# Softmax sums on 32 rows, an earlier start of the input loads, and norms on ScalarE in a four-layer convolution kernel

## The chip, the cores and the metric

The kernel runs on one core of one Trainium2 chip. It is a single program that is launched once; the metric is its device time in microseconds (us), and the time shown for a kernel is the median over several executions. TensorE (PE in the profile) multiplies matrices out of the on-chip buffer SBUF into the accumulator memory PSUM; VectorE (DVE), ScalarE (ACT) and GpSimd (POOL) do elementwise work; SyncE (SP) issues most DMA transfers between the chip's main memory and SBUF. Each engine takes its instructions in the order of its own queue, and waits at the head of the queue until what the instruction needs is there.

## What is computed

The input is x, 4 images of 384 channels and 64 x 64 positions in float32. Four layers follow, each a group norm (32 groups of 12 channels), a block and a residual addition. The change touches layers 0 and 1 alone; layers 2 and 3 (a gated depthwise block with batch norms, and a depthwise 7 x 7 convolution with kernels made from the data) are the same code before and after.

```python
# layer 0: x = x + L0(group_norm(x))
x_attn, x_skip = x[:, :96], x[:, 96:]
xn  = layer_norm_over_channels(x_attn) * ln_w + ln_b
qkv = bn(einsum('oc,bchw->bohw', w_qkv, xn))          # 16 + 16 + 96 channels
attn = softmax(einsum('bcn,bcm->bnm', q, k) * scale)  # over all 4096 positions
out  = einsum('bcn,bmn->bcm', v, attn)
xm = relu(concatenate([out, x_skip], axis=1))
y  = bn(einsum('oc,bchw->bohw', w_proj, xm))

# layer 1: x = x + L1(group_norm(x))
t = einsum('bchw,oc->bohw', x, w_in)
t = irfft2(rfft2(t in 8 x 8 patches) * fft_filter)
t = depthwise_3x3(t, w_dw)
g = gelu(t[:, :192]) * t[:, 192:]
y = einsum('bchw,oc->bohw', g, w_out)
```

## The kernel before

**Tiling.** The 384 channels lie as NJ = 3 groups of 128 partitions (P), the 4096 positions of an image as eight blocks of 512 columns. One image is called a batch, numbered 0 to 3. The attention works on the first 96 channels (PD), the other 288 are the skip channels.

**The whole program.** `phase_a` does layers 0 and 1, and is what the change edits; layers 2 and 3 follow. `phase_a` first loads constants and weights and makes the projection weights (`qkv_weights`). From these weights a bound on the scores is worked out (`score_bound`); it is compared with a limit, and the result, the one integer `large`, is read into a register in `score_shifts` (L637), where every engine branches on it (L638). Only if it is 1 are the maxima of the scores computed; in the runs here it is 0 and the branch jumps over them. Then `x_norm(0)` loads batch 0 in 24 pieces of 256 KB on SP's queue (L565) and takes its group-norm statistics, and `qkv(0)` makes queries, keys and values. Then, for each batch b, `side_by_side` interleaves the steps of `attention(b)` with `others`: the statistics of batch b+1, layer 1 of batch b-1, and queries, keys and values of batch b+1. Last comes layer 1 of batch 3, which has no attention beside it; the code calls it `alone`, and from its 21st piece on it is interleaved with loads for layer 2 (`strips_of`).

**Order.** The Python order gives each instruction its priority; a tile scheduler then sets the order on each engine, with the scores raised (`high_priority`, L693). Tiles come from pools in which a tag has a number of buffers: a new tile of a tag waits until the oldest one of that tag is no longer read. The PSUM tags are "s" (one tile of four banks: the scores `sc_s`, and in the last batch `taps_m`), "a" (two banks: `av` and `rd_m`; in the last stage the output products `out_m1`) and "m" (two banks: everything taken by `pm`).

**A step of attention.** For query block i and key group c (eight of each), `scores` makes four products of 32 rows each into `sc_s`, and ScalarE takes two exponentials of 128 x 1024 into `probs` (L703). Four products with `vt` add into `av` (L734). `vt` has 97 columns for each 128 keys: 96 value channels and one column of ones, so that row 96 of `av` becomes the softmax's sum. In the products the matrix called weights (loaded into PE first) is `vt`, and `probs` streams through it.

**The end of a block.** One step into the next block (c == 1) `finish(av)` copies `av` through a Relu to `av_up` on ScalarE (L715), VectorE takes the reciprocal of row 96 (L717), PE spreads that one row over 96 rows by a product with a row of ones (`rd_m`, L719), and VectorE multiplies `av_up` with it (L720) into rows 0 to 95 of `xm`. `layer0_end` loads the residual block (`x_res`), fills the skip channels of `xm` on ScalarE (L756, L760), makes nine products for the projection (`proj_m`, L767), adds bias and residual on VectorE (L774), takes statistics and stores the block.

**Layer 1** takes a block of eight rows of the image (a band) as four tiles of 16 columns. For each tile `tile_norm` normalizes three groups on VectorE (L826, `xb`); `tile_hidden` multiplies by w_in (`t_m`, L841) and ScalarE copies (`t_t`, L849); `tile_filter` goes to Fourier coefficients (`coef_m`, L856) and multiplies by the filter on VectorE (L858); `tile_back` goes back (`back_m`, L867) and ScalarE writes the tile into the band (L869). `band_taps` then does the 3 x 3 depthwise convolution: nine taps for each of three groups, tap 0 on ScalarE and eight on VectorE as multiply-and-add (L918). In the `alone` case the first TAPS = 3 taps of a group are made on PE instead, as products with diagonal matrices (L907, built on POOL in `tap_weights`), and VectorE starts from their sum in `taps_m`. Two Gelus and two multiplies give the gate, and `band_out` multiplies by w_out, adds the residual and stores.

**At the start,** `layer_norm` loads a block of x (`ln_x`), normalizes it (L578), centres it by a product, squares it on ScalarE into `ln_rs` (L587; tag "lr", two buffers), averages by a product, takes the root and multiplies. `qkv` then makes `q_m`, `k_m` and the values `v_m` (L625: four products, each with 97 columns of `wv`), copied to `vt` on VectorE (L626).

Of the kernel before, what the change touches and what calls it, by code (L numbers as in the profile page):

```python
# [37 lines left out]
TAPS = 3  # L38
# [187 lines left out]
class _Builder:  # L226
# [154 lines left out]
    def qkv_weights(self, pool):  # L381
# [4 lines left out]
        w = pool.tile([P, PD], F32, tag="wq_raw", name="wq_raw")  # L386
# [7 lines left out]
        wt = pool.tile([PD + 1, P], F32, tag="wq_t", name="wq_t")  # L394
        raw = pool.tile([PD, P], F32, tag="wq_rawt", name="wq_rawt")
# [9 lines left out]
        self.wv = pool.tile([PD + 1, PD + 1], F32, tag="wv", name="wv")  # L405
# [3 lines left out]
        nc.gpsimd.memset(self.wv[PD : PD + 1, PD : PD + 1], 1.0)  # L409
# [28 lines left out]
    def phase_a(self, strips):  # L438
# [3 lines left out]
        with ExitStack() as ctx:  # L442
# [12 lines left out]
            self.one = cp.tile([PD + 1, PD], F32, tag="one", name="one")  # L455
            nc.gpsimd.memset(self.one, 1.0)
            self.w_proj = self.weight(cp, "w_proj_t")
            self.w_in = self.weight(cp, "w_in_t")
            self.w_out = self.weight(cp, "w_out_t")
# [5 lines left out]
            for k in ("r0", "m0", "n0"):  # L465
                setattr(self, k, cp.tile([P, NJ, B], F32, tag=k, name=k))
            w = lambda tag, name: self.work.tile([P, C], F32, tag=tag, name=name)
# [21 lines left out]
            self.qkv_weights(cp)  # L489
            self.score_shifts(cp)  # L490
            for _ in self.x_norm(0):
                pass
# [79 lines left out]
    def layer_norm(self, b, i):  # L572
# [13 lines left out]
        rs = self.wk("ln_rs", "lr", 2)[0:PD]  # L586
# [7 lines left out]
    def qkv_tiles(self):  # L594
# [4 lines left out]
        vt = self.big.tile([P, 32, PD + 1], F32, tag="vt", name="vt", bufs=2)  # L599
        return q, k4, vt  # L600

    def qkv(self, b, q, k4, vt):
# [3 lines left out]
        for i in range(8):  # L606
# [16 lines left out]
            mv = m[:, 0 : 4 * (PD + 1)].rearrange("p (c d) -> p c d", d=PD + 1)  # L623
# [18 lines left out]
    def maxima(self, b):  # L642
# [14 lines left out]
        for i in range(8):  # L657
# [20 lines left out]
            row = self.big.tile([P, 512], F32, tag="up", name="nm_row", bufs=2)  # L678
# [4 lines left out]
    def attention(self, b, q, k4, vt):  # L683
# [27 lines left out]
        def finish(av):  # L711

            xm = self.work.tile([P, NJ, 512], F32, tag="xm", name="xm")
            up = self.big.tile([P, 512], F32, tag="up", name="av_up", bufs=2)[0 : PD + 1]
            nc.scalar.activation(up, av[0 : PD + 1], AF.Relu)  # L715
            rd = self.wk("av_rd", "rd", 1)
            nc.vector.reciprocal(rd[PD : PD + 1], up[PD : PD + 1])  # L717
            m = self.pa("rd_m")
            nc.tensor.matmul(m[0:PD, :], lhsT=self.one[PD : PD + 1, :], rhs=rd[PD : PD + 1], start=True, stop=True)  # L719
            nc.vector.tensor_mul(xm[0:PD, 0], up[0:PD], m[0:PD, :])  # L720
# [58 lines left out]
    def layer1(self, b):  # L779

        nc = self.nc
        r, gm = self.norm1[0:2]
        st = self.stats_tile("x1_st")
        alone = b == B - 1
        if alone:
# [999 lines left out]
```

## Time and profile before

| | |
|---|---|
| median of 9 executions | 5136.43 us (5120.58 to 5146.69) |
| the profiled execution | 5133.12 us, of it the profile's span 5131.4 us |
| TensorE clock granted, mean of the span | 0.947 |
| start, to 80 us: PE busy | 27.7 of 80 us |
| attention of batch 0 (80 to 690): PE, VectorE, ScalarE busy | 593.7, 217.5, 281.1 of 610 us |
| batch 1 (690 to 1230) | 521.7, 283.1, 260.2 of 540 us |
| batch 2 (1230 to 1760) | 511.7, 290.0, 257.8 of 530 us |
| batch 3 (1760 to 2290) | 519.5, 276.8, 236.0 of 530 us |
| layer 1 of batch 3 (2290 to 2610) | 284.0, 205.8, 74.8 of 320 us; clock 0.89 |
| layers 2 and 3 (2610 to the end) | 2199.1, 1394.0, 965.1 of 2521 us; clock 0.92 |

The stages' limits are read from the timeline and rounded to 10 us. In the profile an operation's row names its line, engine, operation, what it writes and what it reads; a trailing x is the number of instructions, "mean ns" the duration of one. Products are pipelined on PE, so durations of one overlap and start-to-start times say more. Between a group's busy time and the next group stands the idle time of the engine just before it and what ended most of that. In the row of slices each digit is the busy share in tenths of one fortieth of the span; PEclk is the granted clock in tenths. In a timeline a row gives start, duration, engine, line and operation, and in brackets the engine's wait before it with the instruction that ended it. In the table of windows each engine has its busy time and its number of instructions, then come granted clock, DMA share and GB/s.

### The profile page before, as it was taken

What the parts mean: (1) busy time and instruction counts of PE and PEld (TensorE: products, weight loads), DVE (VectorE), ACT (ScalarE), POOL (GpSimd) and SP (SyncE); (2) the same over time, 40 slices, a digit from 0 to 9 for tenths busy, and PEclk for the clock granted to TensorE, in tenths of its full rate; (3) what the DMA queues carried; (4) which work ended last, traced back from release to release, by engine and by line L of the source; (5) the groups of instructions that cost most, each with busy time, mean ns of one, the idle gap of its engine ahead of it and who ended that gap; (6) DMA issues with size and microseconds to landing.
All of it is one profiled execution on the core that took longest, in us unless ns stands there. A gap on an engine that the chain in (4) does not pass through costs nothing. (4 is left out here: it accounts for less than half of the span.)

```text
span 5131.4 us, 47956 instructions
## 1 busy us (share of the span) xinstructions
PE 4657.5 (91%) x17963; PEld 2569.1 (50%) x17963; DVE 2703.1 (53%) x4450; ACT 2099.1 (41%) x2753; POOL 733.9 (14%) x524
## 2 busy tenths in 40 slices
PE   5999999999999999999879999599999995559999
PEld 2333444334443343435458888344444442448999
DVE  4322456634555345565767788544421114658775
ACT  3544344454444544443135666311133334652320
POOL 1000000000000000000025555000000000125433
PEclk9999999999999999999979999799999997669999
DMA  5210211111121101113249999766643334647776
GB/s 161 72 48 28 89 56 63 60 51 43 56 71 68 38 31 62 62 68 102 70 127 283 291 297 294 237 257 241 239 180 148 147 136 182 244 161 246 220 221 190
DMA packets 387543, 723.30 MB, mean 141 GB/s; under 512 B 21628, under 2 KB 221159, under 8 KB 380391
## 3 DMA queue, kind: packets, MB, share of 16 engines
q1 hardware_dynamic: 333528, 519.50, 32.4%
q10 hardware_dynamic: 28494, 105.99, 5.2%
q0 software_dynamic: 25280, 94.65, 4.7%
q8 instruction: 145, 2.38, 0.2%
q14 instruction: 96, 0.78, 0.0%
HBM read 432.48 MB, written 287.57 MB: 140 GB/s over the span
## 5 line engine op out<-in xcount | busy, mean ns | idle before, releaser
L734 PE MATMUL av<-probs,vt 128*97 128x512 f32 x2048 | 963.1, 605 | 0.0
L703 ACT ACTIVATE probs<-sc_s 128x1024 f32<-128x1024 f32 x512 | 499.5, 1020 | 758.1 <-PE av L734 741.0
L734 PEld LDWEIGHTS av<-probs,vt 128*97 128x97 f32 x2048 | 321.7, 166 | 508.7 <-issue 505.3
L1123 PE MATMUL conv_m<-toep,z 128*128 128x256 f32 x2304 | 519.9, 385 | 12.9 <-DVE toep L1104 7.4
L918 DVE SCALAR_TENSOR_TENSOR acc<-band,vecs,acc 128x512 f32<-128x512 f32 x696 | 493.1, 746 | 42.6 <-POOL band L879 25.0
L1393 PE MATMUL h_m<-f_h,cm_w_t 128*128 128x512 f32 x1152 | 496.5, 594 | 7.9 <-ACT f_h L1383 7.9
L1123 PEld LDWEIGHTS conv_m<-toep,z 128*128 128x128 f32 x2304 | 438.7, 193 | 74.6 <-DVE z L1057 4.9
L1104 POOL TENSOR_TENSOR toep<-w,band 128x1536 f32<-128x1536 f32 x96 | 330.5, 3444 | 278.4 <-PE conv_m L1123 207.9
L1344 PE MATMUL h_s<-e_tok,cm_w_t 128*128 128x512 f32 x768 | 365.2, 599 | 5.4 <-DVE e_tok L1329 5.4
L1677 PE MATMUL conv_m<-toep,z 128*128 128x128 f32 x3072 | 364.2, 277 | 2.1 <-DVE rest_o L1685 2.1
L1393 PEld LDWEIGHTS h_m<-f_h,cm_w_t 128*128 128x128 f32 x1152 | 219.4, 191 | 284.9 <-issue 272.7
L1677 PEld LDWEIGHTS conv_m<-toep,z 128*128 128x128 f32 x3072 | 355.3, 194 | 2.6 <-issue 2.3
L695 PE MATMUL sc_s<-q,k 32*128 32x512 f32 x2048 | 301.0, 645 | 16.3 <-ACT probs L703 11.5
L841 PE MATMUL t_m<-w_in_t,xb 128*128 128x384 f32 x768 | 283.6, 502 | 6.4 <-ACT band L869 3.2
L1351 ACT COPY e_h<-h_s 128x1024 f32<-128x1024 f32 x96 | 97.2, 1012 | 419.0 <-PE h_s L1344 419.0
L767 PE MATMUL proj_m<-xm,w_proj_t 128*128 128x512 f32 x576 | 264.8, 598 | 0.8 <-DVE xm L720 0.8
L774 DVE SCALAR_TENSOR_TENSOR x_res<-proj_m,bn_c,x_res 128x512 f32<-128x512 f32 x96 | 71.8, 748 | 337.1 <-PE proj_m L767 337.0
L1344 PEld LDWEIGHTS h_s<-e_tok,cm_w_t 128*128 128x128 f32 x768 | 147.8, 193 | 192.1 <-issue 185.4
L1353 DVE BATCH_NORM_STATS2 h_st<-e_h 128x6 f32<-128x512 f32 x192 | 123.2, 685 | 185.7 <-ACT e_h L1351 185.6
L1401 DVE BATCH_NORM_STATS2 h_st<-f_h 128x6 f32<-128x512 f32 x72 | 50.0, 694 | 323.0 <-ACT f_h L1400 323.0
L841 PEld LDWEIGHTS t_m<-w_in_t,xb 128*128 128x128 f32 x768 | 142.0, 193 | 149.7 <-issue 66.1
L1344 PE MATMUL h_s<-z,cm_w_t 128*128 128x512 f32 x384 | 198.2, 599 | 12.1 <-DVE z L1329 12.1
(366 smaller groups left out, 6273.0 us busy)
## 6 DMA issues: line engine op xcount, KB each, us to landing
d<-d_o ACTq DMA_DIRECT2D x96, 512.0 KB
c_d<-d SPq DMA_DIRECT2D x96, 512.0 KB
hid<-e_h ACTq DMA_DIRECT2D x16, 3072.0 KB
f_h<-hid SPq DMA_DIRECT2D x16, 3072.0 KB
x_res<-in_x SPq DMA_DIRECT2D x32, 768.0 KB
x_in<-in_x SPq DMA_DIRECT2D x96, 256.0 KB
xa<-x_res POOLq DMA_DIRECT2D x32, 768.0 KB, 3.9
xa_in<-xa SPq DMA_DIRECT2D x32, 768.0 KB
```

Of the source, the lines that this page charges most:

```text
L695: nc.tensor.matmul(s[:, g], lhsT=k4[32 * g : 32 * g + 32, c], rhs=q[i][32 * g : 32 * g + 32], start=True, stop=True,)
L703: nc.scalar.activation(p[:, h * 1024 : (h + 1) * 1024], s[:, 2 * h : 2 * h + 2].rearrange("p a b -> p (a b)"), AF.Exp, scale=0.25,)
L734: nc.tensor.matmul(av[0 : PD + 1, :], lhsT=vt[:, 4 * c + v, :], rhs=p[:, v * 512 : (v + 1) * 512], start=c == 0 and v == 0, stop=c == 7 an ...
L767: nc.tensor.matmul(m, lhsT=self.w_proj[:, j, o * P : (o + 1) * P], rhs=xm[:, j], start=j == 0, stop=j == NJ - 1,)
L841: nc.tensor.matmul(m[:, 0:C], lhsT=xb[:, j], rhs=self.w_in[:, j, :], start=j == 0, stop=j == NJ - 1,)
L918: nc.vector.scalar_tensor_tensor(out, src(j, k), w, done, ALU.mult, ALU.add)
L1104: eng.tensor_tensor(t, self.w53[:, at : at + 192].rearrange("p (m n) -> p m n", n=8).unsqueeze(2).to_broadcast([P, 24, 8, 8]), band.rearra ...
L1123: nc.tensor.matmul(m[:, c * 256 : (c + 1) * 256], lhsT=self.z_[:, at : at + P], rhs=t[:, 12 * c + 4 * i : 12 * c + 4 * i + 4].rearrange("p ...
L1344: nc.tensor.matmul(s[:, v, :], lhsT=w1[:, j, o * P : (o + 1) * P], rhs=t[j][:, v * 512 : (v + 1) * 512], start=j == 0, stop=j == NJ - 1,)
L1353: nc.vector.bn_stats(st[:, o, 8 * b + 2 * i + v, :], h[:, o, v * 512 : (v + 1) * 512])
L1393: nc.tensor.matmul(m, lhsT=w2[:, o, j * P : (j + 1) * P], rhs=h[:, o, v * 512 : (v + 1) * 512], start=o == 0, stop=o == 5,)
L1677: nc.tensor.matmul(m[:, ch * P : (ch + 1) * P], lhsT=self.z_[:, at : at + P], rhs=t[:, 8 * c + 2 * i : 8 * c + 2 * i + 2].rearrange("p m a ...
```

## The change

It has three parts.

- **Softmax's end.** `wv` and `vt` get 128 columns in place of 97; the columns 96 to 127 are all ones, so that rows 96 to 127 of `av` all hold the softmax's sum. `finish` takes the reciprocal of these 32 rows straight from PSUM, and three multiplies with a maximum against 0 (one for each 32 rows of values) write `xm`. The Relu copy `av_up`, the product `rd_m` and the matrix `one` go. `ln_rs` has one buffer in place of two, and scratch tiles of `qkv_weights` and `maxima` use buffers of the work pool.
- **Start.** `qkv_weights` comes first, then `x_norm(0)` with its 24 loads, then `score_shifts` with the branch, and only then the loads of w_proj, w_in and w_out and the work on the filter and on w_proj.
- **Layer 1 of the last batch.** `tile_norm` uses a ScalarE activation (scale and bias per partition) in place of VectorE's subtract-and-multiply, and TAPS goes from 3 to 2: per group two taps on PE and seven on VectorE.

```diff
@@ -35,7 +35,7 @@
-TAPS = 3
+TAPS = 2
@@ -383,7 +383,7 @@
         nc = self.nc
-        w = pool.tile([P, PD], F32, tag="wq_raw", name="wq_raw")
+        w = self.wk("wq_raw", "lx", 2)[:, 0:PD]
         nc.scalar.dma_start(w, self.ins["w_qkv"])
@@ -391,8 +391,8 @@
         nc.tensor.transpose(pt[0:PD, 0:P], w, self.ident)
-        wt = pool.tile([PD + 1, P], F32, tag="wq_t", name="wq_t")
-        raw = pool.tile([PD, P], F32, tag="wq_rawt", name="wq_rawt")
+        wt = self.wk("wq_t", "ln", 2)[0 : PD + 1, 0:P]
+        raw = self.wk("wq_rawt", "lx", 2)[0:PD, 0:P]
         nc.vector.tensor_copy(raw, pt[0:PD, 0:P])
@@ -402,11 +402,11 @@
         self.wk4 = pool.tile([PD + 1, 4, 32], F32, tag="wk4", name="wk4")
-        self.wv = pool.tile([PD + 1, PD + 1], F32, tag="wv", name="wv")
+        self.wv = pool.tile([PD + 1, P], F32, tag="wv", name="wv")
         for t in (self.wq4, self.wk4, self.wv):
             nc.gpsimd.memset(t, 0.0)
         nc.gpsimd.memset(self.wk4[PD : PD + 1, :, 0:1], 1.0)
-        nc.gpsimd.memset(self.wv[PD : PD + 1, PD : PD + 1], 1.0)
+        nc.gpsimd.memset(self.wv[PD : PD + 1, PD:], 1.0)
         for g in range(4):
@@ -452,11 +452,6 @@
             self.to_pos = self.const(cp, "to_pos")
-            self.one = cp.tile([PD + 1, PD], F32, tag="one", name="one")
-            nc.gpsimd.memset(self.one, 1.0)
-            self.w_proj = self.weight(cp, "w_proj_t")
-            self.w_in = self.weight(cp, "w_in_t")
-            self.w_out = self.weight(cp, "w_out_t")
@@ -464,6 +459,13 @@
                 setattr(self, k, cp.tile([P, NJ, B], F32, tag=k, name=k))
+            self.qkv_weights(cp)
+            for _ in self.x_norm(0):
+                pass
+            self.score_shifts(cp)
+            self.w_proj = self.weight(cp, "w_proj_t")
+            self.w_in = self.weight(cp, "w_in_t")
+            self.w_out = self.weight(cp, "w_out_t")
             w = lambda tag, name: self.work.tile([P, C], F32, tag=tag, name=name)
@@ -486,10 +488,6 @@
                 nc.vector.tensor_mul(self.w_proj[:, j], self.w_proj[:, j], m[:, 0:C])
-            self.qkv_weights(cp)
-            self.score_shifts(cp)
-            for _ in self.x_norm(0):
-                pass
             q, k4, vt = self.qkv_tiles()
@@ -583,7 +581,7 @@
         nc.gpsimd.memset(xn[PD : PD + 1], 1.0)
-        rs = self.wk("ln_rs", "lr", 2)[0:PD]
+        rs = self.wk("ln_rs", "lr", 1)[0:PD]
         nc.scalar.activation(rs, xn[0:PD], AF.Square)
@@ -596,7 +594,7 @@
         k4 = self.big.tile([P, 8, P], F32, tag="k4", name="k4", bufs=2)
-        vt = self.big.tile([P, 32, PD + 1], F32, tag="vt", name="vt", bufs=2)
+        vt = self.big.tile([P, 32, P], F32, tag="vt", name="vt", bufs=2)
         return q, k4, vt
@@ -620,7 +618,7 @@
             m = self.pm("v_m")
-            mv = m[:, 0 : 4 * (PD + 1)].rearrange("p (c d) -> p c d", d=PD + 1)
+            mv = m.rearrange("p (c d) -> p c d", d=P)
             for c in range(4):
@@ -675,7 +673,7 @@
                 )
-            row = self.big.tile([P, 512], F32, tag="up", name="nm_row", bufs=2)
+            row = self.wk("nm_row", "rd", 1)
             nc.scalar.copy(row[0:1], m[0:1])
@@ -711,13 +709,11 @@
             xm = self.work.tile([P, NJ, 512], F32, tag="xm", name="xm")
-            up = self.big.tile([P, 512], F32, tag="up", name="av_up", bufs=2)[0 : PD + 1]
-            nc.scalar.activation(up, av[0 : PD + 1], AF.Relu)
             rd = self.wk("av_rd", "rd", 1)
-            nc.vector.reciprocal(rd[PD : PD + 1], up[PD : PD + 1])
-            m = self.pa("rd_m")
-            nc.tensor.matmul(m[0:PD, :], lhsT=self.one[PD : PD + 1, :], rhs=rd[PD : PD + 1], start=True, stop=True)
-            nc.vector.tensor_mul(xm[0:PD, 0], up[0:PD], m[0:PD, :])
+            nc.vector.reciprocal(rd[PD:P], av[PD:P])
+            for g in range(3):
+                at = slice(32 * g, 32 * g + 32)
+                nc.vector.scalar_tensor_tensor(xm[at, 0], av[at], 0.0, rd[PD:P], ALU.max, ALU.mult)
             return xm
@@ -732,7 +728,7 @@
                 nc.tensor.matmul(
-                    av[0 : PD + 1, :],
+                    av,
                     lhsT=vt[:, 4 * c + v, :],
@@ -781,9 +777,8 @@
         nc = self.nc
-        r, gm = self.norm1[0:2]
         st = self.stats_tile("x1_st")
-        alone = b == B - 1
+        norm, alone = self.norm1, b == B - 1
         if alone:
@@ -792,7 +787,7 @@
                     x = self.block("xa_in", self.xa[b], (n + 2) // 4, bufs=1)
-                xb[n + 2] = self.tile_norm(x, (n + 2) % 4, r, gm)
+                xb[n + 2] = self.tile_norm(x, (n + 2) % 4, norm, alone)
             if n < 0:
@@ -819,18 +814,18 @@
-    def tile_norm(self, x, w, r, gm):
-
+    def tile_norm(self, x, w, norm, alone):
+
+        r, gm, n, _ = norm
         xb = self.work.tile([P, NJ, P], F32, tag="xb", name="xb", bufs=4)
         for j in range(NJ):
-            self.nc.vector.tensor_scalar(
-                xb[:, j].rearrange("p (r c) -> p r c", c=16),
-                x[:, j].rearrange("p (r w c) -> p w r c", w=4, c=16)[:, w],
-                gm[:, j : j + 1],
-                r[:, j : j + 1],
-                ALU.subtract,
-                ALU.mult,
-            )
+            at = slice(j, j + 1)
+            out = xb[:, j].rearrange("p (r c) -> p r c", c=16)
+            src = x[:, j].rearrange("p (r w c) -> p w r c", w=4, c=16)[:, w]
+            if alone:
+                self.nc.scalar.activation(out, src, AF.Identity, bias=n[:, at], scale=r[:, at])
+            else:
+                self.nc.vector.tensor_scalar(out, src, gm[:, at], r[:, at], ALU.subtract, ALU.mult)
         return xb
     def tile_hidden(self, xb):
```

## The prediction

> **What bounds the kernel now.** I read the slices of the page first, then the rows of lines and shapes for the first 2700 us, then the timelines of the three places that the change touches.
>
> ```profile
> PE 4657.5 (91%) x17963; PEld 2569.1 (50%) x17963; DVE 2703.1 (53%) x4450; ACT 2099.1 (41%) x2753; POOL 733.9 (14%) x524
> PE   5999999999999999999879999599999995559999
> PEclk9999999999999999999979999799999997669999
> ```
>
> A slice is 128 us. Attention with layer 1 of earlier batches fills the slices up to about 2290 us, and PE is at 9 in all but the first; VectorE and ScalarE never are. So up to there a PE instruction that goes takes its slot with it, unless PE then waits for something else. The timeline of PE shows such a slot:
>
> ```profile
> 289.59 1.88 PE L734 MATMUL av<-probs,vt 128*97 128x512 f32 x4
> 291.40 1.09 PE L719 MATMUL rd_m<-av_rd,one 1*96 1x512 f32 x2
> 292.43 1.96 PE L734 MATMUL av<-probs,vt 128*97 128x512 f32 x4
> ```
>
> Start to start, the spreading product rd_m takes 292.43 - 291.40 = 1.03 us in a row without waits. The rows of the softmax's end over the whole of it (busy us, mean ns, then idle time before them):
>
> ```profile
> L717 DVE RECIPROCAL av_rd<-av_up 1x512 f32<-1x512 f32 x32 | 107.2, 3349 | 71.2 <-ACT av_up L715 70.6
> L719 PE MATMUL rd_m<-av_rd,one 1*96 1x512 f32 x64 | 36.8, 656 | 4.0 <-DVE av_rd L717 4.0
> L720 DVE TENSOR_TENSOR xm<-av_up,rd_m 96x512 f32<-96x512 f32 x32 | 21.8, 681 | 87.3 <-PE rd_m L719 87.2
> ```
>
> PE lost only 4.0 us waiting for the reciprocal; VectorE lost 71 and 87 us around it, but VectorE is not the bound there. The last batch's layer 1 (2290 to 2610 us) has no attention beside it; PE's timeline there, one band of eight rows:
>
> ```profile
> 2498.51 2.10 PE L841 MATMUL t_m<-w_in_t,xb 128*128 128x384 f32 x6
> ...
> 2502.81 2.20 PE L841 MATMUL t_m<-w_in_t,xb 128*128 128x384 f32 x6 [0.65 <-ACT band L869]
> 2505.64 0.91 PE L856 MATMUL coef_m<-t_t,to_coef 128*128 128x384 f32 x2 [0.62 <-ACT t_t L849]
> 2507.55 1.10 PE L907 MATMUL taps_m<-band,diag 128*128 128x512 f32 x2 [1.00 <-DVE acc L918]
> ```
>
> The bracket is PE's wait. PE waits 2.27 us of a 30.4 us period (the same tap group ends at 2498.5 and at 2528.9); the last wait is for VectorE to have read the one taps_m tile. At the start, VectorE and the SP queue:
>
> ```profile
> 20.87 0.15 DVE L435 TENSOR_SCALAR large<-gram_m 1x1 int32<-1x1 f32 x1 [0.37 <-PE gram_m L433]
> 26.45 15.68 SPq L565 DMA_DIRECT2D x_in<-in_x  x24
> 59.23 0.98 DVE L578 TENSOR_SCALAR ln_x<-ln_x,m,r 96x512 f32<-96x512 f32 x2
> ```
>
> The branch value is written at 21.02; the loads of x come after the branch at 26.45, the first normalized block at 59.23.
>
> **The softmax's end, 32 blocks.** Removed: on PE rd_m, 1.03 us; on ScalarE the Relu copy (L715), 596 ns. VectorE had 3.35 + 0.68 = 4.03 us and gets a reciprocal on 32 rows by 512 columns out of PSUM and three multiply-with-max on 32 rows. The reciprocal's row is for one partition; time goes with the 512 columns (a copy of 32 rows by 128 takes 286 ns, one of 96 rows by 512 takes 684), so 3.35 us stands; the multiplies are like L774, 748 ns from PSUM. Sum 3.35 + 3 x 0.75 = 5.6 us, 1.6 more, 50 us in all, on an engine that is 53% busy and that waited 158 us in these groups. From the end of av the chain was 0.60 + 3.35 + 1.03 + 0.68 = 5.7 us and is 5.6 now. Behind it on VectorE queue the taps of layer 1. By the program's order the projection comes 20 to 32 us of PE work after av's end in 28 blocks, so xm is not awaited there; in the last block of each of the four batches it comes 3 to 6 us after, PE waits for the chain of 5.7 us with rd_m's slot inside it, and I count nothing. av's bank is held for 5.6 us in place of 0.6; two banks alternate every eight steps of at least 4.7 us, so nobody waits. Gain 28 x 1.03 = 29 us; bounds 25 (some slots go to waits for the exponentials) and 32 x 1.03 = 33.
>
> **Wider weights.** av's matrix has 128 columns in place of 97. av moves 512 columns either way; proj_m with 128 weight columns is paced at 0.43 us each, exactly as av is now: 0. The value product v_m (L625) moves 128 columns in place of 97: eight take 0.95 us warm (263.92 to 264.87), 0.119 each; back_m, 128 by 128, takes 0.78 for six, 0.130 each. 256 x 0.011 = 3; if all 31 columns cost in proportion, 256 x 0.119 x 31/97 = 10. I take 4, nearer the row of the same shape. The copy to vt grows from 562 towards 690 ns, 4 us on VectorE, beside PE.
>
> **One buffer in place of two for ln_rs.** The second Square at 67.95 starts before the multiply of the first (68.07 to 68.76); it would start 0.8 us later. In the steady rhythm the multiply ends at 95.66 and the next Square starts at 102.79: no cost. So 0.8 for each of four starts at most, 3 us; I take 1, since only batch 0 has no attention to cover it.
>
> **The start.** The 24 loads of x come on SP right after to_pos (issued by 9.54), 17 us earlier than 26.45, and ahead of pick and two loads of x_res, which nothing needs before the branch. Before, loads and statistics took 26.45 to 49.2. Now they share the transfers with 1.57 MB of weights; 6.3 MB in 22.8 us is 276 GB/s, so up to 5.7 us more. I take 3: last statistics at 9.5 + 22.8 + 3 = 35.3. To the norm's copies took 9.5 us before (49.2 to 58.7): 44.8. Now the branch follows: 21.02 to 25.83 (POOL) or 26.45 (SP) is 4.8 to 5.4 us: 49.9. Behind it, on the path, stand the filter's copy (0.55) and three multiplies of w_proj (1.47): 51.9 against 59.23, a gain of 7.3. If PE's filter and row products (1.65 each) are not over by then, or the weights take all, it is 1; if sharing costs nothing, 10. I take 6.
>
> **The last batch's layer 1.** Each band loses three of nine tap products on PE: 3 x 0.857 = 2.6 us; VectorE gets three taps of about 0.66 us start to start (L918, 746 ns with overlap) and loses twelve norms of 0.28 to 0.34. By the built order twelve accumulations stand ahead of the read that frees taps_m, in place of ten: the third wait above grows by 2 x 0.66 = 1.3 us to 2.3. So a band gains 2.6 if PE's work is the bound and 1.3 if that loop is; five periods between bands give 6 to 13, middle 9.5. In the last bands two rows' taps now stand ahead of the output products, and the wait of 3.93 us for taps_m at 2550.8 mostly goes (3 us); the final tap products shrink from 18 to 12 instructions at half clock (10.31 to 6.9 us), against 3.3 us more of VectorE's chain: 0 to -1. The norms on ScalarE: no row has the shape; the row with two operands per partition is 804 ns for 512 columns (L760) and 1236 for 1024 (L1074), which on a line gives 0.48 for 128; bounds 0.26 (three columns, L311) and 0.80. Twelve are 5.8 us per band on an engine with 5.2 of 30 us, behind the copies that PE awaits. I take 11 in all, 5 to 17.
>
> Sum: -29 + 4 + 1 - 6 - 11 = -41. The profiled execution took 5133.1 us (span 5131.4), 3.3 under the median 5136.4; on the median's scale 5136 - 41 = **5095 us**. Its own bounds: -33 + 0 + 0 - 10 - 17 = -60, 5076, and -25 + 10 + 3 - 1 - 5 = -18, 5118; all ends at once are unlikely.
>
> **Rivals.** *The clock falls in each band of the last batch.* In one band of the last stage the same three waits were followed by half clock:
>
> ```profile
> 2470.00:2475.00 5.00, 3.20 (x9) 1.35 (x8) 5.00 (x9) 1.61 (x3) 0.00 (x0) 1.00 0.00 2
> 2475.00:2480.00 5.00, 4.53 (x8) 2.02 (x9) 5.00 (x11) 0.00 (x0) 0.00 (x0) 0.66 0.01 3
> ```
>
> The clock column (third from the end) is 0.66, and four output products took 3.32 us where they take 1.88 at 2508.48: 1.5 to 1.7 us lost. In two other bands with the same waits it stayed 1.00. With 3.6 us of waits in place of 2.3 it could fall in every band: 7 x 1.7 = 12 back, 5107. The Trainium skill ("TensorE: Matmul & The Clock Gate", "What's actually happening") says that a free-running window of about 3.4 us decides, and that an idle one halves the clock; by that rule the longer waits make the fall likelier, and the one fall in three bands agrees. *PE's slot is refilled.* A step's scores, exponentials and next scores take 4.68 us (164.51 to 169.19), as long as PE's own work of it, so PE could wait for the exponentials where rd_m stood. Against it: steps with inserted work last longer by just that work, and PE's waits for probs between 700 and 2160 us are 6.9 us in all. Then -29 becomes 0: 5124. *ScalarE's norms hold PE up (slower).* PE turns through two PSUM tiles in t_m, coef_m and back_m, freed in part by ScalarE's copies; a tile takes PE 3.50 us (2330.51 to 2334.01), ScalarE 0.98 plus 1.44 for three norms, 2.4. Where strips are loaded ScalarE has 13.6 of 25 us; with 4.4 more, 18. It decides when ScalarE's share of a tile passes 3.5, or a norm waits ahead of a copy; if every tile then grew by its norms, 32 x 1.44 = 46: -29 + 4 + 1 - 6 + 46 = +16, 5152. *The early loads bring nothing* (weights first, branch behind the norm): 5101, inside my range.
>
> **Chances.** Forecast, with its own bounds, 62%; more than that (VectorE's freed waits) 4%; clock 13%; early loads void 7%; slot refilled 7%; ScalarE 7%. Range for 8 in 10: from 5072, a little beyond the lower bound, to 5120, which holds forecast, clock and void loads. The measurement tells about 0.2%, 10 us, from no change: the refilled slot lies on that border and gives the 6% for the same; slower is the 7% of ScalarE's case; faster 87%.
>
> **What would show it.** Right: no rd_m; PE at 9 in the same slices, attention's end some 30 us earlier than 2282; av still paced at 0.43; the first ln_x at 52 to 58; taps_m with 96 PE instructions; bands 28 to 29 us apart. Wrong: PE idle before probs or proj_m at xm; reciprocals far from 3.35 us; PE waiting at t_t or band for ScalarE by more than 0.7; clock under 1.00 in each band; first ln_x after 59.

## The result and the profile after

| | before | after |
|---|---|---|
| median, us | 5133.8 (45 executions) | 5110.3 (15) |
| ratio of the two | | 0.996, 95% interval 0.9951 to 0.9969 |
| span of the profiled execution, us | 5131.4 | 5107.6 |

The kernel became 23.5 us faster, 0.46%. The forecast was 41 us faster, 5095 us, with a range of 5072 to 5120: the measured time lies inside it, and the gain is a little over half of the one forecast. The page of the kernel after:

```profile
PE 4619.2 (90%) x17851; PEld 2619.7 (51%) x17851; DVE 2746.0 (54%) x4442; ACT 2117.7 (41%) x2817; POOL 732.2 (14%) x520
PE   5999999989999999999879999599999995559999
PEclk9999999999999999999979999799999997559999
```

PE lost 38 us of busy time, yet the span fell by only 24: PE waits more. The first slice below 9 in the attention stands at 1020 to 1150 us (the 8), where batch 1 ends and the layer norm of batch 2 runs.

Four landmarks on PE cut the span into stages: the first scores, the last `av`, the first `conv_m` of layer 2, the end.

| stage, us | before | after | change | forecast |
|---|---|---|---|---|
| to the first scores | 76.3 | 68.5 | -7.8 | -6 |
| attention, to the last `av` | 2205.0 | 2192.2 | -12.8 | -24 |
| layer 1 of the last batch, to `conv_m` | 346.8 | 342.6 | -4.2 | -11 |
| layers 2 and 3, same code | 2503.3 | 2504.3 | +1.0 | 0 |

The same code takes a little longer or shorter from one profiled execution to the next: layers 2 and 3 took 2496.5 to 2509.5 us over all kernels here, the attention of before 2205.0 to 2211.6 us over five kernels that hold it unchanged, and the attention of after 2192.2 to 2201.1 us over four. A single stage of a single profile therefore tells some 9 us, no less, and for the attention the two profiles of the table are the lowest of each kind. Averaged over the kernels below that hold the old and the new code of a stage, the start gained 9.3 us (77.5 to 68.2), the attention 11.1 (2207.3 to 2196.2) and the last batch 4.1 (345.8 to 341.8). These make 24.5 us, close to the measured 23.5.

The rows of lines and shapes of the kernel after, first 2700 us (busy us, mean ns, idle time before and what ended it):

```profile
L713 DVE RECIPROCAL av_rd<-av 32x512 f32<-32x512 f32 x32 | 107.6, 3364 | 96.6 <-PE av L730 96.3
L716 DVE SCALAR_TENSOR_TENSOR xm<-av,av_rd 32x512 f32<-32x512 f32 x96 | 65.6, 684 | 1.9
L826 ACT ACTIVATE xb<-xa_in,gn_n,gn_r 128x128 f32<-128x128 f32 x96 | 41.2, 485 | 3.9 <-DVE gn_n L377 2.9 <-DMA xa_in<-xa 0.9
L763 PE MATMUL proj_m<-xm,w_proj_t 128*128 128x512 f32 x576 | 269.6, 607 | 7.3 <-DVE xm L716 7.3
L587 PE MATMUL ln_v<-ln_rs,mean 96*96 96x512 f32 x64 | 39.8, 708 | 23.9 <-ACT ln_rs L585 21.7 <-DVE x_st L564 2.1
L902 PE MATMUL taps_m<-band,diag 128*128 128x512 f32 x96 | 49.9, 643 | 20.7 <-DVE acc L913 20.7
```

Three of these rows before:

```profile
L767 PE MATMUL proj_m<-xm,w_proj_t 128*128 128x512 f32 x576 | 264.8, 598 | 0.8 <-DVE xm L720 0.8
L589 PE MATMUL ln_v<-ln_rs,mean 96*96 96x512 f32 x64 | 37.3, 666 | 10.9 <-ACT ln_rs L587 10.9
L907 PE MATMUL taps_m<-band,diag 128*128 128x512 f32 x144 | 69.1, 616 | 13.2 <-DVE acc L918 13.2
```

The single operations cost what was forecast: 3.36 us for a reciprocal on 32 rows (forecast 3.35), 684 ns for a multiply (750), 485 ns for a norm on ScalarE (480). What is off stands in the idle column: PE now waits 7.3 us for `xm` at `proj_m` (before 0.8), 23.9 at `ln_v` (before 10.9) and 20.7 at `taps_m` (before 13.2).

**Where the attention's gain went.** Between the first scores and the last `av` PE's time was split into start-to-start time of its products without waits, and waits. The products took 2145.2 us before and 2113.4 after, 31.8 less: `rd_m` had 32.7. The waits went from 59.8 to 78.8 us. By what PE stood in front of: `ln_v` +12.2, `proj_m` +6.5, `back_m` +3.1, group-norm products +3.1, `v_m` +2.5; `sc_s` -4.3, `k_m` -2.5, `t_m` -1.8. The `ln_v` of this before, 7.8 us, is the lowest of five; averaged over the same kernels as above it rose by 10, from 10.4 to 20.3, and all waits together by 20. The slot was not refilled where the rival of the forecast had it (at the scores, waiting for the exponentials): those waits fell. It was refilled where PE waits for chains over VectorE and ScalarE, which do not become shorter because PE has less to do. The timeline of the last block of batch 1, after:

```profile
1128.81 3.37 DVE L713 RECIPROCAL av_rd<-av 32x512 f32<-32x512 f32 x1
...
1132.21 1.19 DVE L619 COPY k<-k_m 32x128 f32<-32x128 f32 x4
1133.41 0.69 DVE L624 COPY vt<-v_m 128x512 f32<-128x512 f32 x1
1134.11 2.08 DVE L716 SCALAR_TENSOR_TENSOR xm<-av,av_rd 32x512 f32<-32x512 f32 x3
1136.34 4.94 PE L763 MATMUL proj_m<-xm,w_proj_t 128*128 128x512 f32 x7 [2.71 <-DVE xm L716]
```

The same place before:

```profile
1143.90 1.09 PE L719 MATMUL rd_m<-av_rd,one 1*96 1x512 f32 x2
1145.69 0.68 DVE L720 TENSOR_TENSOR xm<-av_up,rd_m 96x512 f32<-96x512 f32 x1
1146.43 5.85 PE L767 MATMUL proj_m<-xm,w_proj_t 128*128 128x512 f32 x13 [0.40 <-DVE xm L720]
```

Before, the same two copies ran on VectorE while PE made `rd_m` and two products of `av`, and one multiply of 0.68 us followed; PE waited 0.40 us. Now three multiplies of 2.08 us stand behind the copies, and PE waits 2.71. From the start of the reciprocal to `proj_m` it takes 7.53 us in place of 5.93. The three such blocks inside the attention make the 6.5 us; in the fourth, the last of batch 3, PE waits 6.88 us for VectorE at the output products where it waited 3.97 at `rd_m`.

At `ln_v` the trace explains a part. The layer norm makes a product (`ln_s`), VectorE copies it (`ln_xn`), ScalarE squares the copy, and only then PE can make `ln_v`. A block of it beside the end of a softmax block, after and then before:

```profile
1049.06 3.36 DVE L713 RECIPROCAL av_rd<-av 32x512 f32<-32x512 f32 x1 [0.99 <-PE av L730]
1052.46 0.69 DVE L582 COPY ln_xn<-ln_s 96x512 f32<-96x512 f32 x1
1053.92 1.10 PE L587 MATMUL ln_v<-ln_rs,mean 96*96 96x512 f32 x2 [1.25 <-ACT ln_rs L585]
```

```profile
1064.27 0.69 DVE L584 COPY ln_xn<-ln_s 96x512 f32<-96x512 f32 x1 [2.02 <-PE ln_s L582]
1066.37 3.35 DVE L717 RECIPROCAL av_rd<-av_up 1x512 f32<-1x512 f32 x1 [1.41 <-ACT av_up L715]
```

Before, the reciprocal came behind ScalarE's Relu copy and so behind the layer norm's copy. Now it reads `av` itself, goes first, and the layer norm's copy starts 3.60 us after its product began, in place of 1.06. A wait of this kind, 1.2 to 2.0 us, stands at three places (376, 1054 and 1657 us here), in every kernel with the new softmax end and in none with the old one. So the removed ScalarE copy, which the forecast counted as 0.60 us off the chain, has a price too.

**A band of the last batch,** PE's timeline after:

```profile
2477.82 2.20 PE L836 MATMUL t_m<-w_in_t,xb 128*128 128x384 f32 x6 [0.65 <-ACT band L864]
2480.65 0.91 PE L851 MATMUL coef_m<-t_t,to_coef 128*128 128x384 f32 x2 [0.62 <-ACT t_t L844]
2483.88 1.10 PE L902 MATMUL taps_m<-band,diag 128*128 128x512 f32 x2 [2.32 <-DVE acc L913]
2484.82 3.31 PE L928 MATMUL out_m<-acc,w_out_t 128*128 128x512 f32 x4
```

The same three waits as before, the third 2.32 us in place of 1.00, as forecast. But the four output products behind it take 3.31 us where they take 1.88 at full clock. The windows of the kernel after show why (busy us of PE, PEld, DVE, ACT, POOL, then granted clock, DMA share, GB/s):

```profile
2481.00:2484.00 3.00, 0.68 (x3) 0.15 (x2) 3.00 (x6) 1.38 (x3) 0.00 (x0) 1.00 0.00 0
2484.00:2488.00 4.00, 4.00 (x7) 1.60 (x8) 3.96 (x7) 0.00 (x0) 0.00 (x0) 0.64 0.02 4
```

Between the first tap product and the last, the clock was at half for 3.4 us in five places (at 2352, 2410, 2454, 2485 and 2516 us), before in one (2476); in the last bands it was at half for longer, 13.7 us after and 10.2 before. Four of the five follow this wait at `taps_m`; the one at 2410 follows a wait of 2.29 us for a strip of layer 2. From one band's last tap product to the next one's went 30.9, 34.7, 36.3, 30.9, 30.8, 26.1 and 18.4 us, before 30.5, 36.3, 36.0, 32.1, 30.4, 25.6 and 19.2: but for the 32.1, which holds the one fall of before, a band gained next to nothing.

The Trainium skill ("TensorE: Matmul & The Clock Gate", "HAM oscillation — how this bites in real kernels") gives as the rule that PE have no idle gaps over some 3.4 us. Here the longest gap ahead of one of these five falls is 2.44 us, and in the band shown it is 2.32 with 1.27 us of gaps close before it; the measurement decides. The forecast's reading, that longer waits make the fall likelier, is borne out by the counts at the end of this document. The length of each of the five, 3.41 us, agrees with the window of the section "What's actually happening".

**The start** after, in the timeline:

```profile
8.24 17.92 SPq L563 DMA_DIRECT2D x_in<-in_x  x24
...
45.77 0.82 SPq L575 DMA_DIRECT2D ln_x<-in_x  x2
...
50.57 0.99 DVE L576 TENSOR_SCALAR ln_x<-ln_x,m,r 96x512 f32<-96x512 f32 x2
```

The first normalized block comes at 50.57 (59.23 before, 51.9 forecast). The last statistics end at 32.6, the branch lies between the norms at 41.2 and the next load at 45.8.

### The profile page after: what moved, and what is told of

Its sections match the earlier page's. It is cut to its first block, busy times and chain, and to the rows that moved or that the text cites. A ratio compares the mean times of both kernels' runs of the same rounds, so it can differ in the third digit from the quotient of the medians.

```text
span 5107.6 us, 47804 instructions
## 1 busy us (share of the span) xinstructions
PE 4619.2 (90%) x17851; PEld 2619.7 (51%) x17851; DVE 2746.0 (54%) x4442; ACT 2117.7 (41%) x2817; POOL 732.2 (14%) x520
## 5 line engine op out<-in xcount | busy, mean ns | idle before, releaser
L730 PE MATMUL av<-probs,vt 128*128 128x512 f32 x2048 | 963.5, 605 | 0.0
L701 ACT ACTIVATE probs<-sc_s 128x1024 f32<-128x1024 f32 x512 | 499.9, 1020 | 757.4 <-PE av L730 742.8
L730 PEld LDWEIGHTS av<-probs,vt 128*128 128x128 f32 x2048 | 372.7, 192 | 472.8 <-issue 465.2
L913 DVE SCALAR_TENSOR_TENSOR acc<-band,vecs,acc 128x512 f32<-128x512 f32 x720 | 509.7, 746 | 41.0 <-POOL band L874 25.1
L1339 PE MATMUL h_s<-z,cm_w_t 128*128 128x512 f32 x384 | 197.1, 596 | 11.1 <-DVE z L1324 11.1
```

What stands on the lines that cost most here:

```text
L701: nc.scalar.activation(p[:, h * 1024 : (h + 1) * 1024], s[:, 2 * h : 2 * h + 2].rearrange("p a b -> p (a b)"), AF.Exp, scale=0.25,)
L730: nc.tensor.matmul(av, lhsT=vt[:, 4 * c + v, :], rhs=p[:, v * 512 : (v + 1) * 512], start=c == 0 and v == 0, stop=c == 7 and v == 3,)
L913: nc.vector.scalar_tensor_tensor(out, src(j, k), w, done, ALU.mult, ALU.add)
L1339: nc.tensor.matmul(s[:, v, :], lhsT=w1[:, j, o * P : (o + 1) * P], rhs=t[j][:, v * 512 : (v + 1) * 512], start=j == 0, stop=j == NJ - 1,)
```

## The experiments

Each kernel was timed beside the kernel before on the same chip; the ratio is to that. Stage times come from the profiled executions.

**One part at a time.** Three kernels have one part of the change each. `start`: the four moves in `phase_a` alone. `soft`: the softmax's end, the wide `vt` and `wv`, the single `ln_rs` buffer and the scratch tiles that make room. `last`: the two edits on the last batch.

```diff
# start, against the kernel before
+            self.qkv_weights(cp)
+            for _ in self.x_norm(0):
+                pass
+            self.score_shifts(cp)
             self.w_proj = self.weight(cp, "w_proj_t")
# last, against the kernel before
-TAPS = 3
+TAPS = 2
-                xb[n + 2] = self.tile_norm(x, (n + 2) % 4, r, gm)
+                xb[n + 2] = self.tile_norm(x, (n + 2) % 4, norm, alone)
# soft: the changed kernel with the old order of the start and
-TAPS = 2
+TAPS = 3
-                xb[n + 2] = self.tile_norm(x, (n + 2) % 4, norm, alone)
+                xb[n + 2] = self.tile_norm(x, (n + 2) % 4, norm, False)
```

> The kernel before with the new order of the start alone (loads of x ahead of the branch, weights and filter behind it). Theory A (the start lies on the path and nothing takes it back): first scores at 67 to 69 us in place of 76.3, and the whole 7 to 9 us shorter. Theory B (batch 0's attention gives it back through transfers or waits): first scores early, batch 1's first scores less than 4 us earlier than 525.6, the whole within 3 us of before.

> The kernel before with the softmax's new end, the wide vt and the one ln_rs buffer that it needs; start and last batch as before. Theory A (rd_m's 32 us go, one buffer takes 8 back and the last block of each batch some 6 to 9): the stretch from the first scores to the last av falls from 2205 by 11 to 15 us, the whole likewise. Theory B (PE refills the slot by waiting for the exponentials): waits at sc_s rise by over 10 us. The prediction's sum would be 24 us less.

> The kernel before with the last batch's norms on ScalarE and TAPS 2, nothing else. Theory A (VectorE's nine tap sums, not PE's products, set the band's period, and the longer wait brings the clock down in more bands): the stretch from the last av to conv_m shrinks by 3 to 6 us of 346.8, waits at taps_m rise from 13 us to about 20, the clock falls in 3 to 6 bands. The prediction's: 11 us shorter, waits at taps_m up by 7 as well, but the lost 1.3 us a band being all of it.

Measured:

| | ratio (95% interval) | stage | before | this |
|---|---|---|---|---|
| start | 0.998 (0.997 to 0.999) | first scores | 76.3 | 68.0 |
| soft | 0.9973 (0.9959 to 0.9987) | attention | 2205.0 | 2194.9 |
| last | 0.9988 (0.9978 to 0.9999) | last batch | 346.8 | 340.6 |

The three ratios make 10 + 14 + 6 = 30 us, and with the widths of the intervals that is the 23.5 of the whole. Of the sizes that theory A gave, the first scores of `start` (68.0 us) and the whole of `soft` (14 us) came inside; the whole of `start` (10 us, expected 7 to 9), the attention of `soft` (10.1, expected 11 to 15) and the stretch of `last` (6.2, expected 3 to 6) fell just outside, by less than can be told. Theory B of `start` and of `soft` fell: nothing gave the start back, and the waits at `sc_s` did not rise. In `start` the rest of the program stayed as it was (attention 2207.4). In `soft` PE's waits in the attention are 81.4 us, as in the changed kernel (78.8), with 7.3 at `proj_m` and 20.4 at `ln_v`: the waits belong to this part, not to the moved start. In `last` the waits at `taps_m` are 20.7 us and the clock falls in four places, three of them at `taps_m`. One band shows what the fall costs: its wait of 2.32 us brought no fall, and it took 29.2 us; the next one, with a fall, took 30.7. `lx3` below shows the same pair, 29.2 and 30.8. So without a fall a band gains 1.2 us (30.4 to 29.2), near the 1.3 of the forecast's lower case, and the fall takes them back.

**One buffer for `ln_rs`.** The kernel before with this edit alone:

```diff
-        rs = self.wk("ln_rs", "lr", 2)[0:PD]
+        rs = self.wk("ln_rs", "lr", 1)[0:PD]
```

> The kernel before with one buffer for ln_rs in place of two, nothing else. Theory A (the single buffer puts each next Square behind the multiply of the block before, so PE waits longer at ln_v wherever two blocks of the layer norm follow one another): PE's waits at ln_v over the attention rise from 7.9 us to 15 to 20, the attention's end comes 5 to 9 us later than 2281.3, the whole is 5 to 9 us longer than before. Theory B (the prediction's: it costs the start alone): 1 us, the waits at ln_v stay within 2 us of before.

Measured: ratio 1.0007 (0.9994 to 1.0019). Attention 2207.7 us, inside what five kernels with two buffers show; waits at `ln_v` 12.1 us, where those kernels show 7.8 to 12.6. Theory A, formed after the result, fell in its size: the waits did not come near 15. The whole can't tell 1 us from 9, but the trace shows what the buffer does. With one buffer ScalarE's Square waits 0.75 us for the multiply of the block before at three places, in every kernel here that has it; with two it never does. At the second block of the layer norms of batches 2 and 3 PE's wait at `ln_v` is 3.5 to 4.1 us with one buffer and 2.7 to 3.3 without. By these waits the single buffer costs some 2 to 3 us, and not only at the start.

The reverse was tried on the changed kernel: `lx3` writes `ln_rs` into the tile of `ln_x`, which gets three buffers in the same room.

```diff
-        x = self.wk("ln_x", "lx", 2)[0:PD]
+        x = self.wk("ln_x", "lx", 3)[0:PD]
...
-        rs = self.wk("ln_rs", "lr", 1)[0:PD]
+        rs = x
```

> The changed kernel with ln_rs in the tile of ln_x, which gets three buffers in place of two (as much room): the Square needs no longer wait for the multiply of the block before. Theory A (one buffer costs 3 us, as the run with that edit alone showed, and the rest of the 12 us more at ln_v comes from the order on VectorE): waits at ln_v fall from 20.0 us to 13 to 16, attention 2 to 5 us shorter than 2192.2. Theory B (the single buffer is behind all of it): waits at ln_v back to 8 to 10, attention 8 to 12 us shorter.

Measured: ratio 0.9946 (0.9929 to 0.9963), 5103.0 us; attention 2189.1. That is what theory A forecast, but not for its reason: waits at `ln_v` are 18.9 us (20.0 in the changed kernel), not 13 to 16, and all waits in the attention 81.6 (78.8). The attention is shorter by less half-clock time (54.6 us in place of 68.3), which a second kernel with the same edit (below, 2195.2) does not show again. Over the four kernels with this edit the waits at `ln_v` are 16.0 to 18.9 us, over the four with the single buffer and the new softmax end 20.0 to 20.4. So the buffer is 2 to 3 of the 10 us that came there, and most of them have another cause. The interval of `lx3` overlaps that of the changed kernel: that it is faster isn't shown.

**The last block of each batch.** `prio` raises the reciprocal and the multiplies of each batch's last block on VectorE.

```diff
+            with tc.high_priority() if last else ExitStack():
                 nc.vector.reciprocal(rd[PD:P], av[PD:P])
                 for g in range(3):
```

> The changed kernel with the reciprocal and the three multiplies of each batch's last block put ahead on VectorE by priority. Theory A (in the last block xm is awaited, and the copies of k and vt that stand between the reciprocal and the multiplies, 1.9 us, are the wait): PE's waits at proj_m fall from 7.3 us to 2 to 4, attention 3 to 5 us shorter than 2192.2. Theory B (the wait only moves, to the copies of k and vt or to the products of layer 1): waits in the attention within 2 us of 78.8.

Measured: ratio 0.9964 (0.9952 to 0.9976), as the changed kernel's; waits at `proj_m` 7.7 us, in the attention 83.0. The timeline of `prio` at the same block:

```profile
1131.96 3.37 DVE L714 RECIPROCAL av_rd<-av 32x512 f32<-32x512 f32 x1
...
1135.35 0.28 DVE L619 COPY k<-k_m 32x128 f32<-32x128 f32 x1
1135.64 2.08 DVE L717 SCALAR_TENSOR_TENSOR xm<-av,av_rd 32x512 f32<-32x512 f32 x3
1137.75 0.90 DVE L619 COPY k<-k_m 32x128 f32<-32x128 f32 x3
...
1138.80 4.51 PE L764 MATMUL proj_m<-xm,w_proj_t 128*128 128x512 f32 x6 [2.87 <-DVE k L619]
```

`xm` is now ready before the last copies of k, and PE waits as long as before, for these copies: `proj_m` takes one of the two "m" banks, and both are held by `k_m` and `v_m` until VectorE has copied them. Theory B held: the wait only moved. VectorE's work ahead of `proj_m` is 6.6 us here (3.37 + 0.28 + 2.08 + 0.90) in place of 7.3 (3.37 + 1.19 + 0.69 + 2.08). The 0.7 us do not show in the wait, because two products of `av` instead of four stand ahead of `proj_m` on PE.

**The two edits of the last batch apart.** `norms` has the norms on ScalarE with TAPS 3, `taps2` has TAPS 2 with the norms on VectorE.

> The kernel before with the last batch's norms on ScalarE, TAPS still 3. Theory A (VectorE's sums set a band's period: in the run with both edits waits at taps_m were 20.7 us against 13.2): VectorE loses 3.5 us a band and gains nothing, so waits at taps_m fall below 8 us, the clock falls in no more than 1 of the bands, and the stretch from the last av to conv_m shrinks by 8 to 16 us of 346.8, more than the 6.2 of both edits together. Theory B (ScalarE's norms hold PE up at t_t and band, as the slower rival of the prediction had it): waits at coef_m, t_m and back_m rise from 5.9 us to over 15, the stretch does not shrink.

> The kernel before with TAPS 2 alone, norms still on VectorE. Theory A (VectorE is the longer of the two in a band): PE's products fall by 18 us, waits at taps_m rise by more than 15 us over 13.2, the clock falls in 4 or more bands, the stretch from the last av to conv_m is 0 to 12 us longer than 346.8. Theory B (PE's products set the period): 8 to 12 us shorter.

Measured: `norms` 1.0004 (0.9993 to 1.0015), last batch 345.0 us, waits at `taps_m` 13.0, one fall of the clock of 3.4 us; `taps2` 1.0001 (0.9991 to 1.0011), 343.1 us, waits 20.8, five such falls. Theory A was wrong in both, but for the five falls of `taps2`; so was theory B of `taps2`, 8 to 12 us shorter. VectorE lost twelve norms a band and nothing came of it: the waits at `taps_m` are 13 us with TAPS 3 and 21 with TAPS 2, wherever the norms are. In a band of `norms` VectorE stands idle for 6.32 us until the tap products are there, then makes its two first sums and ten accumulations in a row, and only then reads the third group. PE and VectorE take turns on one tile. That this is what sets the band is shown by the next kernel. Theory B of `norms`, ScalarE holding PE up, fell too: waits at `coef_m`, `t_m` and `back_m` are 7.8 us, 5.9 before.

**A tile for each group's taps.** `rot` is the changed kernel with four tiles of one PSUM bank in place of one tile of four banks, so that a group of the next band waits for the read of its own bank alone.

```diff
+            self.psum_t = ctx.enter_context(tc.tile_pool(name="psum_t", bufs=4, space=bass.MemoryType.PSUM))
...
-            m = self.p4("taps_m")
+            m = []
             for j in range(NJ):
+                m.append(self.psum_t.tile([P, 512], F32, tag="t", name="taps_m", bufs=4))
                 for k in range(TAPS):
-                    nc.tensor.matmul(m[:, j], lhsT=self.diag[j][:, k], rhs=src(j, k), ...)
+                    nc.tensor.matmul(m[j], lhsT=self.diag[j][:, k], rhs=src(j, k), ...)
```

The scores' tile of four banks moves into a pool of its own that is closed after the attention.

> The changed kernel with each group's tap products in a PSUM tile of its own, four of one bank in place of one of four, so that the next band's first group needs no read of this band's last group. Theory A (PE waits for the one tile, 12 accumulations behind in place of 10 since TAPS is 2, and the wait of 2.3 us brings the clock to half in four or five bands): waits at taps_m fall from 20.7 us to under 8, the clock falls in 0 or 1 band, the stretch from the last av to conv_m gets 10 to 20 us shorter than 342.6. Theory B (VectorE's chain is the period whatever the tile): under 4 us shorter, PE waits elsewhere.

Measured: 5080.0 us, ratio 0.99 (0.988 to 0.9921). The row of the tap products and the window of one band in `rot`:

```profile
L907 PE MATMUL taps_m<-band,diag 128*128 128x512 f32 x96 | 45.9, 595 | 0.0
```

```profile
2441.00:2466.00 25.00, 25.00 (x81) 12.63 (x80) 19.48 (x30) 9.60 (x22) 2.01 (x5) 1.00 0.39 131
```

No wait at `taps_m`, PE busy in all of 25.00 us at full clock, and a band every 24.9 us in place of 30.9. Of these 6 us the clock is 1.5: with the one tile and without a fall a band took 29.2. The last stretch took 308.6 us in place of 342.6: 34 us, more than the 10 to 20 expected. Two further kernels with this edit (below) show 308.6 and 309.2, four with the one tile and both edits of the last batch 339.6 to 344.2. The attention of this profile, 2201.1 us, is the longest of the four with the same code; 78.5 us of it were at half clock, in the changed kernel 68.3. Of the 34 us, 25 are waits (62.2 to 37.3); the other 9 are products that ran at full clock (the taps 4.3 us less, `back_m` 2.0, four others about 1 each, two about 1 more). It was more than expected because the tile had also set the last bands: the last two gaps between tap ends went from 26.1 and 18.4 us to 20.1 and 5.2. The Trainium skill ("Perfetto Trace Analysis", "Optimizing Tensor Performance") advises that independent groups of products rotate through different PSUM banks, so that reading one overlaps the next one's products. The groups lay in different banks before; what held them together was that they were one tile.

**On top of both repairs.** `lx3_rot` has `lx3` and `rot` together, `lx3_rot1` also has TAPS 1, and `lx3_rot_k` makes the copies of k of a batch's last two blocks on ScalarE.

> Both repairs together: ln_rs in the tile of ln_x with three buffers, and tap sums in tiles of their own. If the two are independent, the gains add: attention as in the run with the first alone (2189), the last stretch as in the run with the second alone; the whole 10 to 20 us below 5110. If either comes only from a chance order of the instructions, they do not add.

> As the run with both repairs, with TAPS 1: one tap of a group on PE, eight on VectorE. Theory A (with the wait on the tile gone PE's own work is the band's period): a band gets 2 to 2.6 us shorter and the last stretch 10 to 18 us shorter than with TAPS 2. Theory B (VectorE's 24 accumulations, 16 us, with what else it has, are then the longer part): not shorter, or longer by up to 10 us.

> As the run with both repairs, with the copies of k of the last two blocks of a batch on ScalarE, so that between the reciprocal and the multiplies of a batch's last block stands vt's copy alone, 0.7 us in place of 1.9. Theory A (these copies hold back xm, and the bank that proj_m needs): waits at proj_m fall from 7.3 us to about 5 or less and the attention gets 2 to 4 us shorter. Theory B (ScalarE, which makes the layer norm's roots, only passes the wait on): within 2 us.

| | median, us | ratio (95% interval) | attention | last batch |
|---|---|---|---|---|
| lx3_rot | 5073.6 | 0.9884 (0.9866 to 0.9903) | 2195.2 | 309.2 |
| lx3_rot1 | 5067.8 | 0.9871 (0.9851 to 0.9892) | 2196.2 | 305.4 |
| lx3_rot_k | 5077.7 | 0.9889 (0.9872 to 0.9906) | 2195.7 | 308.6 |

The whole of `lx3_rot` lies 37 us under 5110, more than the 10 to 20 expected, because `rot` gave more than expected. The intervals of `rot` and `lx3_rot` overlap, so whether `lx3` adds anything is open. With TAPS 1 the last batch gained 4 us and not 10 to 18: PE lost 20 us of tap products, but its waits rose from 38.5 to 54.8 us, most at the output products, which wait for VectorE's sums (18.9 to 31.5). That is between the two theories. The copies of k on ScalarE did little: waits at `proj_m` 6.6 in place of 7.3, the whole the same. The trace shows the same as in `prio`: from the start of the reciprocal to `proj_m` it takes 6.33 us in place of 7.53, but two products of `av` less stand ahead of it on PE. All three beat both kernels clearly.

## Why the prediction was right, and where it was wrong

The sum came out inside its range because the range was wide: the start gave 2 to 3 us more than its term, the attention about half of its term, and the last batch less than half.

**The start: right, in part by luck.** 7.8 us in place of 6 (9.3 on average). The loads' end (35.3 us forecast, 32.6 measured) and the norms' copies (44.8 forecast, 41.2 measured) came early, and the branch took 4.5 us, about as forecast. But from the branch to the first normalized block 4.9 us passed in place of 2.0, because VectorE waited for PE's filter and row products (over at 47.6 and 49.1 us), which the forecast had named as the condition of its lower case. The two errors nearly cancel. That nothing gave the start back is shown by `start`.

**Softmax's end: right in its mechanism, wrong in its size.** The products of the attention fell by 31.8 us, as forecast. The step that failed is "in the last block of each of the four batches it comes 3 to 6 us after ... and I count nothing", and beside it the 28 slots taken as gained. The chain was compared as 5.7 against 5.6 us without what stands between its parts on VectorE's queue. There the copies of k and `vt` had been hidden under `rd_m`; now they and two more multiplies are in line, and PE waits 6.5 us more, which neither another order (`prio`) nor copies of k on ScalarE (`lx3_rot_k`) took away. The rest of the 19 us, 12.2 of it at `ln_v`, lies where the next batch's layer norm runs beside the attention. By batches, from one's first scores to the next one's: -2.7, -1.2, -3.6 and -5.3 us, of some 8 us of `rd_m` in each; averaged over the kernels with the same attention -2.9, -2.3, -0.3 and -5.6. Batch 3, which has no next batch beside it, kept most; what batches 1 and 2 kept lies inside the scatter of the profiles. The layer norm passes from PE to VectorE, to ScalarE and back, and its chain does not become shorter because PE has less to do. Of the 10 to 12 us at `ln_v` the single buffer is 2 to 3, and the reciprocal that now goes ahead of the layer norm's copy 3 to 4 (three waits of 1.2 us); the latter is read from the trace, no kernel turned the two around. Most of the rest lies in batch 0, where the waits went from 2.4 to 8.6 us. What sets the pace there (statistics of the next batch that stand ahead of the copy of `ln_s` on VectorE, for one) was not tried and stays open.

**Wider weights: right, with a smaller price.** `av` is paced as before (921.6 and 921.1 us for its 2048 products); `v_m` took 1.0 us more where 4 was taken.

**One `ln_rs` buffer: inside its bounds, but not where it was put.** The forecast had no cost in the steady rhythm and 1 us at the start; the traces show the Square held up at the start and in the layer norms of batches 2 and 3, 2 to 3 us in all, at the term's upper bound of 3.

**The last batch: wrong in size, by a rival that came true.** The step that failed is "a band gains 2.6 if PE's work is the bound and 1.3 if that loop is; five periods between bands give 6 to 13, middle 9.5". The loop is the bound: the wait did grow by 1.3 us, and `last` shows 1.2 us of gain in a band without a fall of the clock. The falls then took 1.5 us of each band in which they came. This was the clock rival, put at 13% and 5107 us. That the measured 5110 lies nearer to it than to the forecast is luck: it took 12 us back by falls in all bands, and four more falls of 1.5 us make 6, while the attention fell short by more. The forecast had both numbers, a wait that grows to 2.3 us and one fall in three bands at shorter waits, and priced them apart. In the last bands the tail hardly shrank either, since the wait for the one tile grew there too (8.88 to 10.13 us).

**ScalarE's norms: right.** 485 ns each, and no wait for ScalarE that matters.

## What to carry to other kernels

A product taken away from the busiest engine is worth its slot only where that engine's next work is ready; where it waits for a chain over other engines, the slot comes back as a wait there, so the stage's waits have to be listed before the slot is counted. When a wait recurs at one tile, ask first what releases the tile: splitting the one tile of taps into four gave 34 us of its stage, more than all three parts of the change, and moving VectorE's norms away gave nothing. An operation that becomes ready earlier on an engine's queue can hold up another chain there, as the reciprocal did here. A wait that grows by a microsecond beside other waits can cost a second time through the clock.

## What the hardware showed unexpectedly

PE's clock fell to half for 3.4 us after waits of 0.65, 0.62 and 2.32 us within 7 us, although no single gap was near 3.4 us. Whether it fell went with the length of the last wait: in the five profiles with one tile and TAPS 2, 18 of the 20 waits of 2.0 to 2.5 us at `taps_m` were followed by a fall; in these and the five profiles with TAPS 3, 4 of the 29 waits of 0.2 to 1.6 us were.
